# Four convolution layers on one core: chains that use the shared bank in turns, and layer 2's edge columns taken from the loaded chunk

## The chip, the core and the metric

The kernel runs on one core of a Trainium2 chip. The metric is the device time of one execution in microseconds. Before the change three runs took 2754.84, 2755.46 and 2756.58 us; the median is 2755.46 us.

A core has five engines, each with its own queue of instructions that it takes strictly in order: PE (TensorE, the matrix products), DVE (VectorE), ACT (ScalarE), POOL (GpSimd) and SP (SyncE, which here only issues DMA transfers; POOL issues some too). Engines wait for one another through semaphores. PE writes to PSUM, whose banks hold 512 single-precision numbers for each of 128 partitions; DVE and ACT read PSUM, POOL does not.

## The reference

The input `x` has 16 images of 64 channels and 128 x 128 pixels. Four residual layers follow one another, the first three with a group normalization of 32 groups (two channels each), all in single precision:

```python
# --- layer 0: product with the Gram matrix of the normalized image
x = x + _L0_conv_ref(_gn(x), L0_conv_conv_w)   # gram = xf xf^T / N; conv_w (gram xf)
# --- layer 1: |gx| + |gy| of a 3 x 3 Sobel-like filter, channel by channel
x = x + _L1_conv_ref(_gn(x))
# --- layer 2: shift a quarter of the channels left and a quarter right by one column, then a 3 x 3 convolution with bias
x = x + _L2_conv_ref(_gn(x), L2_conv_W, L2_conv_b)
# --- layer 3: 3 x 3 convolution, 1 x 1 convolution, batch normalization over all images, clipped to 0..255
x = x + _L3_conv_ref(_gn(x), ...)
```

`_gn` subtracts a group's mean and divides by its standard deviation, which need the whole image. So each layer of an image waits for sums over the layer before it. The batch normalization of layer 3 needs all 16 images.

## The kernel before

**Tiling.** An image is cut into `NS` = 8 chunks of `R` = 8 rows in each half; a tile has 128 partitions, two times 64 channels. The layers run as software-pipelined stages: `Gram` (the Gram matrix), `Front` (layers 0 and 1), `Layer2` and `Layer3`. A main loop goes over steps, each of four quarters `q` = 0 to 3. In each quarter every stage's `at(i, q)` issues its part of chunk `i`. `Front` starts image `b` at step 15 + 8 b, `Layer2` at 25 + 8 b, `Layer3` at 35 + 8 b, so the three work side by side on different images, and an image takes eight steps. In a quarter Layer3 comes first, then Layer2, then Front. The helper `InOrder` keeps every engine's instructions in the order in which the program issues them: what the code says first on an engine is done first on it.

**Chains.** The scalar work between layers (means, inverse standard deviations, the folded weights of layer 0) is written as Python generators: `gram_chain` for an image's Gram matrix and `coefficients` for the normalizations before layers 2 and 3. `tick()`, called at the end of each quarter, moves every live chain on to its next `yield`. A chain alternates small DVE operations with small products on PE (`small_product`); `rstd` also takes a square root on ACT, named `sd`. The products' results lie in one PSUM bank, `bank`; `sm(n)` hands out its columns. The Gram matrices of the images after the sixth accumulate in the same bank. Reads and writes of the bank by two engines are kept in program order, whichever columns they touch. A Gram chain of a late image waits, after its first DVE read, until step 8 b - 4; its last result, `lead[b]`, is taken by `Front` 13 steps after step 8 b.

**Layer 2.** `load(i + 2)` in quarter 1 fetches a chunk of layer 1's output on SP's queue into a tile `v2` (the profile calls it `v`), shifting the channels by one column on the way. The flat tile is `self.whole[i]`; `self.v[i]` is the part from its second element on. A step later, in quarter 1, ACT normalizes the whole tile in place (`act.activation(f, f, ...)`; `v<-v,co` in the profile). POOL then computes the edge columns that the shift loses: four `tensor_scalar_mul` operations of 64 x 8 elements (`edges<-v,co`), and after them two multiplications by the masks `keep0` and `keep1` on 128 x 9 elements (`v<-v,kc`). The convolution uses differences of rows (`d`, by DVE) and copies of them shifted by a column (`qd`, the `twin`). In layer 2 the twin is made by two DMA transfers on POOL's queue, `twin(0)` in quarter 0 and `twin(1)` at the end of quarter 3. PE computes a shared product (`one`, a single PSUM buffer), which ACT copies to `c`, and two own products (`two`). DVE adds the edges to `two` with two operations of 8 elements a partition, then adds `c` and takes the sum (`x<-two,c`). The sums of squares are ACT's (`junk`).

**Layer 3** has the same form with its own `one`, `two`, `c`, `d`, `qd` (copied by ACT) and `y<-two,c`. **Front** does layer 0 on PE (`po`), normalizes on ACT into `xh`, and computes the Sobel part on DVE (`u`, `e`), with the absolute values on ACT (`u<-u`, `e<-e`). While Gram products run, ACT also turns rows of `x` into columns (`xw<-xr`).

After the last image the batch normalization's sums are finished, and a tail loads layer 3's result and layer 2's output, normalizes, clips, adds and stores.

In the functions below, the change touches `tick`, `coefficients`, `gram_chain` and `Layer2.at`, and adds `when` and `Layer2.sides`.

Of the kernel before, what the change touches and what calls it, by code (L numbers as in the profile page):

```python
# [108 lines left out]
def tile_kernel(ctx: ExitStack, tc: tile.TileContext, x, cw_h, w2_t, b2, wbin_t, w1_t, b1, gamma, beta, consts, out):  # L109
# [143 lines left out]

    now = [0]
    chains = []

    def tick():
        for c in list(chains):
            if next(c, chains) is chains:
                chains.remove(c)  # L260
# [19 lines left out]
    def coefficients(st, put, back=None):  # L280

        s2 = sv("s2", 2)
        dve.tensor_reduce(s2, st, axis=AX.X, op=ALU.add)
        yield
        pm = sm(2)
        small_product(pm, k("gmean"), s2)
        yield
        co = sv("co", 2) if back is None else sv("co2", 6)
        me = sv("me", 2)
        r, mean = co[:, 0:1], me[:, 0:1]  # L290
        yield from rstd(pm, r, me, GN_EPS)
        dve.scalar_tensor_tensor(co[:, 1:2], mean, -1.0, r, op0=ALU.mult, op1=ALU.mult)
        if back is not None:

            dve.reciprocal(co[:, 2:3], r)
            dve.tensor_mul(co[:, 3:4], co[:, 2:3], k("left"))
            dve.tensor_mul(co[:, 4:5], co[:, 2:3], k("right"))
            dve.tensor_add(co[:, 5:6], mean, back)
        put(co)


# [2 lines left out]
    def gram_chain(b, pg):  # L304

        gs = stp.tile([P, C + 1], F32, tag="gs", name=f"gs_{b}", bufs=2)
        if b > 2 * EARLY:
            dve.tensor_reduce(gs, pg.rearrange("p (j c) -> p c j", j=3), axis=AX.X, op=ALU.add)
        else:
            dve.tensor_copy(gs, pg)  # L310
        if b > 1:
            yield
        while b > 2 * EARLY and now[0] < NS * b - 4:
            yield
        gd = sm(C + 1)
        small_product(gd, k("same"), gs)
        yield
# [9 lines left out]
        )  # L327
        if b > 1:
            yield
        pm = sm(2)  # L330
        small_product(pm, k("gavg"), st)
        yield
# [9 lines left out]
            dve.tensor_scalar_mul(dd[:, s, :], k("Id"), vv[:, s:s + 1])  # L342
        if b > 1:
            yield

        pr = sm(2 * C)
        small_product(pr, k("all"), dd.rearrange("p s c -> p (s c)"))
# [9 lines left out]
        csf = cs.rearrange("p s c -> p (s c)")  # L357
        if b > 1:
            yield
        pq = sm(C)  # L360
        small_product(pq, csf, rc)
        yield
# [8 lines left out]
        dve.tensor_add(abd, wbd, k("I"))  # L371
        if b > 1:
            yield
        pd = sm(C + 3)
        small_product(pd[:, 0:C], csf, ad)
        small_product(pd[:, C:C + 2], abd, vv[:, 0:2])
# [7 lines left out]
        dve.tensor_copy(av, pd[:, C:C + 3])  # L384
        if b > 1:
            yield
        pk = sm(1)
        small_product(pk, pp.rearrange("p s c -> p (s c)"), k("q"))
        if b > 1:
# [8 lines left out]
        )  # L398
        if b > 1:
            yield  # L400
        pm = sm(2)
        small_product(pm, k("gavg"), st1)
        yield
# [343 lines left out]
    class Layer2:  # L747
# [7 lines left out]
        def load(self, i):  # L755
# [14 lines left out]
            self.v[i] = t[:, 1:N - 1].rearrange("p (j w) -> p j w", w=W)  # L770
            self.whole[i] = t

        def store(self, i):

            d, t = x3_d[self.b], tiles3[self.b][i]
            for s in range(2):
                v = pairs(d, 1)[:, i * R:(i + 1) * R, :].rearrange("c (n s) w -> c s n w", s=2)
                sp.dma_start(v[:, s], t[hi, s])
            for s in range(2):
                j = i * R + 1 + s  # L780
                m = CP if i + 1 < NS or s == 0 else CP - 1
                if j + 2 * m <= NP:
                    v = pairs(d, 0)[:, j:j + 2 * m, :].rearrange("c (n s) w -> c s n w", s=2)[:, 0]
                else:
                    v = pairs(d, 0)[:, j - 1:j - 1 + 2 * m, :].rearrange("c (n s) w -> c s n w", s=2)[:, 1]
                sp.dma_start(v, t[lo, s, 0:m])
            if i + 1 == NS:
                sp.dma_start(pairs(d, 0)[:, 0:1, :], t[lo, 1, CP - 1:CP])
# [24 lines left out]
        def at(self, i, q):  # L813
# [3 lines left out]
            if q == 0:  # L817
                if i == NS:
                    chains.append(coefficients(self.st, self.done))
                if 1 <= i:  # L820
                    two = self.p.pop(i - 1)[0]

                    e = self.edges.pop(i - 1).rearrange("p t (m n) -> p t n m", n=2)
                    for side, w in ((0, 0), (1, W - 1)):
                        dve.tensor_add(two[:, :, :, w], two[:, :, :, w], e[:, side])
                    x3 = ring.tile([P, 2, CP, W], F32, tag="x3", name=f"x3_{b}_{i - 1}", bufs=NS + 2)
                    tiles3[b].append(x3)
                    dve.scalar_tensor_tensor(
                        x3.rearrange("p s j w -> p s (j w)"), two.rearrange("p s j w -> p s (j w)"), 1.0,
                        self.c.unsqueeze(1).to_broadcast([P, 2, CP * W]),  # L830
                        op0=ALU.mult, op1=ALU.add, accum_out=self.st[:, 0, i - 1:i],
                    )
                if 0 <= i < NS:
                    difference("d2", 0, self.v[i], m)
                    self.twin(0)
            if q == 1:
                if i == 0:

                    self.wi = stp.tile([P, 2, 3, P], F32, tag="wi", name=f"wi_{b}", bufs=1)
                    for n, base in ((0, w2[:, 2]), (1, wm)):  # L840
                        dve.scalar_tensor_tensor(
                            self.wi[:, n].rearrange("p k o -> p (k o)"), k("I3"), self.co[:, 2:3],
                            base.rearrange("p k o -> p (k o)"), op0=ALU.mult, op1=ALU.add,
                        )
                if -1 <= i < NS - 1:
                    if i == -1:
                        self.co = coefs2.pop(b)
                    t, f = self.v[i + 1], self.whole.pop(i + 1)
                    act.activation(f, f, AF.Identity, bias=self.co[:, 1:2], scale=self.co[:, 0:1])


                    e = stp.tile([P, 2, R], F32, tag="edges", name=f"edges_{b}_{i + 1}", bufs=3)
                    for side, at in ((0, 0), (1, W + 1)):
                        for rows, j in ((lo, 1), (hi, 0)):
                            n = at + j * W
                            pool.tensor_scalar_mul(
                                e[rows, side], f[rows, n:n + (R - 1) * W + 1:W], self.co[rows, 3 + side:4 + side]
                            )
                    self.edges[i + 1] = e

                    pool.tensor_scalar_mul(t[:, :, 0], t[:, :, 0], k("keep0"))
                    pool.tensor_scalar_mul(t[:, :, W - 1], t[:, :, W - 1], k("keep1"))
                if i + 2 < NS:
                    self.load(i + 2)
# [28 lines left out]
                        issue([taps(0, p, [w2[:, 0], both], srcs), taps(1, p, [both, w2[:, 1]], srcs)])  # L893
            if q == "first of 3" and 0 <= i < NS:
                self.c = ring.tile([P, CP * W], F32, tag="c2", name=f"c2_{b}_{i}", bufs=1)
                act.activation(self.c, flat(self.p[i][1]), AF.Identity, bias=self.co[:, 5:6])
            if q == "last of 0" and i == NS:
                self.square(i - 1)
            if q == "last of 3" and -1 <= i < NS - 1:
                difference("d2", 1, self.v[i + 1], CP if i + 2 < NS else CP - 1)  # L900
                self.twin(1)


    class Layer3:
# [266 lines left out]
```

## Time and profile before

| what | value |
|---|---|
| median of three runs | 2755.46 us |
| the profiled execution's own time | 2756.86 us |
| its span, first to last instruction | 2755.1 us |
| busy: PE, DVE, ACT, POOL | 2159.6, 2192.4, 2113.5, 943.2 us |
| mean granted clock of PE | 0.896 |
| HBM traffic | 346.23 MB read, 268.44 MB written |
| the `edges` operations on POOL | 512, in all 397.7 us, 0.30 us the shortest, 0.32 the median, 4.46 the longest |
| the edge additions on DVE | 256, 171 ns in the mean |

The profile is of one execution. Busy time is the time in which an engine has an instruction under way; matmuls are pipelined, so PE's is only roughly the time of its work. A wait row tells who waited, for whom, the total in us, the number of times, and the longest. A timeline row tells when an instruction starts, how long it takes, its engine, its output and inputs by the program's names, its shape and how many equal ones were merged; in brackets stands how long the engine was idle before it and what ended that. All instructions of the ordered engines bear one line number, that of the helper, so the names of the tiles tell them apart.

### The profile page before, as it was taken

To read this page: it belongs to the slowest core of one execution; us is meant where nothing else is said; L and a number is where in the kernel's file an instruction comes from. 1 tells how busy PE (TensorE), PEld (TensorE's weight loads), DVE (VectorE), ACT (ScalarE), POOL (GpSimd) and SP (SyncE) were. 2 spreads that over 40 slices of the span, in tenths; PEclk is the share of its full clock that TensorE was granted. 3 is DMA by queue.
4 is the path that set the end of the run, shared out by engine and by line. 5 is a ranking of instruction groups with operands and counts; after the bars stand their busy time and mean duration, and the time that the engine had idled before them with its cause. 6 is when DMAs were issued, how large, how long until landed. Compare 5 with 4: busy or idle time off the path is not lost. (4 is left out here: it accounts for less than half of the span.)

```text
span 2755.1 us, 46091 instructions
## 1 busy us (share of the span) xinstructions
PE 2159.6 (78%) x14804; PEld 886.9 (32%) x14804; DVE 2192.4 (80%) x3623; ACT 2113.5 (77%) x3177; POOL 943.2 (34%) x1350
## 2 busy tenths in 40 slices
PE   6578799999999999999999999999999994000000
PEld 4233333434343434343434343333334641000000
DVE  4998899899999999999999999999996335333332
ACT  4766779998989898989898989899997667333332
POOL 2055444444444444444434444454544300000000
PEclk8689899999999999999999999999999997555555
DMA  8799779898888898888888887888887768999999
GB/s 206 200 229 233 196 183 249 214 244 220 235 224 233 215 240 224 234 227 224 230 228 226 223 203 192 208 207 206 216 207 192 219 191 297 419 420 420 420 420 384
DMA packets 693601, 685.96 MB, mean 249 GB/s; under 512 B 60096, under 2 KB 580448, under 8 KB 693360
## 3 DMA queue, kind: packets, MB, share of 16 engines
q1 hardware_dynamic: 668208, 613.83, 76.0%
q0 software_dynamic: 25152, 69.18, 9.9%
q8 instruction: 119, 1.95, 0.3%
q14 instruction: 122, 1.00, 0.1%
HBM read 346.23 MB, written 268.44 MB: 223 GB/s over the span
## 5 line engine op out<-in xcount | busy, mean ns | idle before, releaser
L73 PE MATMUL two<-d,w 128*64 128x508 f32 (+2 forms) x2560 | 837.5, 587 | 0.0
L73 PE MATMUL two<-d,wi 128*64 128x508 f32 (+3 forms) x1536 | 572.7, 578 | 0.0
L73 POOL DMA_DIRECT2D qd<-d x512 | 270.8, 531 | 851.5 <-issue 295.8
L73 PE MATMUL two<-qd,pk 128*64 128x512 f32 (+1 forms) x1024 | 518.3, 587 | 10.1 <-DMA qd<-d 8.8
L73 POOL TENSOR_SCALAR edges<-v,co 64x8 f32<-64x8 f32 x512 | 397.7, 777 | 287.4 <-ACT v L73 204.0
L73 DVE TENSOR_TENSOR d<-v 128x512 f32<-128x512 f32 (+1 forms) x512 | 346.5, 679 | 58.4 <-issue 29.7
L73 PE MATMUL one<-v,w 128*64 128x508 f32 (+2 forms) x1600 | 364.6, 580 | 30.1 <-ACT c L73 30.1
L73 PEld LDWEIGHTS two<-d,w 128*64 128x64 f32 x2560 | 265.8, 136 | 326.3 <-issue 289.8
L73 PE MATMUL one<-v,wi 128*64 128x508 f32 (+3 forms) x1536 | 360.6, 602 | 1.5 <-issue 1.4
L73 ACT COPY qd<-d 64x512 f32<-64x512 f32 x512 | 315.5, 616 | 18.6 <-DVE d L73 12.5
L73 DVE SCALAR_TENSOR_TENSOR e<-e 128x1032 f32<-128x1032 f32 (+1 forms) x256 | 313.2, 1223 | 0.0
L73 ACT ACTIVATE xh<-po,co 128x128 f32<-128x128 f32 (+1 forms) x480 | 274.9, 621 | 31.0 <-PE po L73 24.9
L73 POOL TENSOR_SCALAR v<-v,kc 128x9 f32<-128x9 f32 x256 | 246.7, 976 | 11.9
L73 ACT ACTIVATE u<-u 128x1024 f32<-128x1024 f32 x128 | 135.7, 1060 | 144.2 <-DVE u L73 144.2
L73 PEld LDWEIGHTS two<-d,wi 128*64 128x64 f32 x1536 | 177.5, 136 | 193.5 <-issue 179.2
L73 ACT ACTIVATE v<-x,co 128x512 f32<-128x512 f32 (+2 forms) x368 | 235.0, 705 | 0.0
L73 DVE SCALAR_TENSOR_TENSOR y<-two,c 128x1024 f32<-128x1024 f32 x128 | 156.0, 1219 | 94.0 <-ACT v L73 68.2
L73 PE MATMUL po<-x,abd 64*64 64x512 f32 (+1 forms) x1024 | 177.7, 641 | 43.9 <-ACT xh L73 41.6
L73 PEld LDWEIGHTS one<-v,w 128*64 128x64 f32 x1600 | 124.6, 136 | 227.9 <-issue 139.5
L73 PEld LDWEIGHTS two<-qd,pk 128*64 128x64 f32 x1024 | 136.0, 136 | 151.1 <-issue 101.9
L73 DVE SCALAR_TENSOR_TENSOR u<-xh 128x1170 f32<-128x1170 f32 x128 | 175.4, 1371 | 4.8 <-ACT xh L73 4.5
L73 PEld LDWEIGHTS one<-v,wi 128*64 128x64 f32 x1536 | 109.3, 139 | 195.9 <-issue 188.3
(165 smaller groups left out, 3321.0 us busy)
## 6 DMA issues: line engine op xcount, KB each, us to landing
x<-in_x SPq DMA_DIRECT2D x256, 256.0 KB, 4.6
x_d<-u SPq DMA_DIRECT2D x512, 128.0 KB, 4.0
y_d<-y SPq DMA_DIRECT2D x512, 128.0 KB, 3.8
x_d<-x SPq DMA_DIRECT2D x496, 128.0 KB, 2.8
xr<-in_x SPq DMA_DIRECT2D x120, 512.0 KB, 6.5
qd<-d POOLq DMA_DIRECT2D x256, 130.0 KB, 3.1
qd<-d POOLq DMA_DIRECT2D x256, 129.8 KB, 3.9
v<-x_d SPq DMA_DIRECT2D x448, 72.1 KB, 2.9
```

Of the source, the lines that this page charges most:

```text
L73: return self.tc.keep_in_program_order(call(*args, **kwargs))
```

## The change

**Turns.** `tick` counts quarters. `when(who)` holds a chain until the count has the right parity: DVE's reads of the bank by the Gram chain start in odd ticks (quarters 0 and 2), the small products in even ones (quarters 1 and 3). All of `gram_chain` from the third image on is put in these turns, and the product in `coefficients`. In `gram_chain` the loop that waits for step 8 b - 4 moves ahead of the first `yield`.

**Edges.** The edge columns are computed from the loaded chunk as it is, before it is normalized: (value - mean) times a mask, in one POOL operation, where before the normalized value was multiplied by a coefficient. The coefficients of layer 2 have five columns for six: the mean is kept, and the two masked inverses go. `sides(i)` does the four POOL operations. For chunk 0 it is called in quarter 0 of the step before the image's first, for the others at the end of quarter 3, one step after the load was issued. The normalization stays in quarter 1 and works in place, so it comes after `sides` of its chunk; the mask multiplications stay behind it. On DVE one operation over both edge columns adds the edges where there were two.

```diff
+    turn_of = [0]
+    VECTOR, TENSOR = 1, 0
+    def when(who):
+        while turn_of[0] % 2 != who:
+            yield
     def tick():
+        turn_of[0] += 1
         for c in list(chains):
...
         dve.tensor_reduce(s2, st, axis=AX.X, op=ALU.add)
         yield
+        yield from when(TENSOR)
         pm = sm(2)
...
             dve.reciprocal(co[:, 2:3], r)
-            dve.tensor_mul(co[:, 3:4], co[:, 2:3], k("left"))
-            dve.tensor_mul(co[:, 4:5], co[:, 2:3], k("right"))
-            dve.tensor_add(co[:, 5:6], mean, back)
+            dve.tensor_copy(co[:, 3:4], mean)
+            dve.tensor_add(co[:, 4:5], mean, back)
...
+        if b > 1:
+            yield from when(VECTOR)
         if b > 2 * EARLY:
             dve.tensor_reduce(gs, pg.rearrange("p (j c) -> p c j", j=3), axis=AX.X, op=ALU.add)
         else:
             dve.tensor_copy(gs, pg)
+        while b > 2 * EARLY and now[0] < NS * b - 4:
+            yield
         if b > 1:
             yield
-        while b > 2 * EARLY and now[0] < NS * b - 4:
-            yield
+            yield from when(TENSOR)
         gd = sm(C + 1)
         small_product(gd, k("same"), gs)
...
+        def sides(self, i):
+            e = stp.tile([P, 2, R], F32, tag="edges", name=f"edges_{self.b}_{i}", bufs=3)
+            for side, at, which in ((0, 0, "left"), (1, W + 1, "right")):
+                for rows, j in ((lo, 1), (hi, 0)):
+                    n = at + j * W
+                    pool.tensor_scalar(
+                        e[rows, side], self.whole[i][rows, n:n + (R - 1) * W + 1:W], self.co[rows, 3:4],
+                        k(which)[rows], op0=ALU.subtract, op1=ALU.mult,
+                    )
+            self.edges[i] = e
...
-                    e = self.edges.pop(i - 1).rearrange("p t (m n) -> p t n m", n=2)
-                    for side, w in ((0, 0), (1, W - 1)):
-                        dve.tensor_add(two[:, :, :, w], two[:, :, :, w], e[:, side])
+                    e = self.edges.pop(i - 1).rearrange("p t (m n) -> p n m t", n=2)
+                    ends = two[:, :, :, 0:W:W - 1]
+                    dve.tensor_add(ends, ends, e)
...
+            if q == 0 and i == -1:
+                self.co = coefs2.pop(b)
+                self.sides(0)
             if q == 1:
...
                 if -1 <= i < NS - 1:
-                    if i == -1:
-                        self.co = coefs2.pop(b)
                     t, f = self.v[i + 1], self.whole.pop(i + 1)
                     act.activation(f, f, AF.Identity, bias=self.co[:, 1:2], scale=self.co[:, 0:1])
-                    e = stp.tile([P, 2, R], F32, tag="edges", name=f"edges_{b}_{i + 1}", bufs=3)
-                    for side, at in ((0, 0), (1, W + 1)):
-                        for rows, j in ((lo, 1), (hi, 0)):
-                            n = at + j * W
-                            pool.tensor_scalar_mul(
-                                e[rows, side], f[rows, n:n + (R - 1) * W + 1:W], self.co[rows, 3 + side:4 + side]
-                            )
-                    self.edges[i + 1] = e
                     pool.tensor_scalar_mul(t[:, :, 0], t[:, :, 0], k("keep0"))
...
             if q == "last of 3" and -1 <= i < NS - 1:
                 difference("d2", 1, self.v[i + 1], CP if i + 2 < NS else CP - 1)
                 self.twin(1)
+                if i + 2 < NS:
+                    self.sides(i + 2)
```

The other places where `yield from when(TENSOR)` goes in are the six further products of `gram_chain`, each after its `yield`.

## The prediction

> **What bounds the kernel now.** I read the granted clock first (0.896 over the span, 1.00 from 500 to 2110 us), then the busy time by stretches, then the waits of each engine, then the timeline of single passes. The columns of the stretches are length, then busy time and instructions of PE, PEld, DVE, ACT and POOL, clock, DMA share, GB/s.
>
> ```profile
> 150.80:500.00 349.20, 302.49 (x2312) 123.75 (x2309) 317.25 (x579) 268.46 (x403) 167.42 (x214) 0.93 0.86 217
> 500.00:1700.00 1200.00, 1177.58 (x8314) 466.24 (x8312) 1143.63 (x1944) 1098.86 (x1716) 520.89 (x746) 1.00 0.86 225
> 2310.00:2755.00 445.00, 0.00 (x0) 0.00 (x0) 154.44 (x128) 154.60 (x127) 0.00 (x0) 0.50 1.01 413
> ```
>
> Three engines are over 90% busy in the middle: PE 98%, DVE 95%, ACT 92%. PE is the bound there, VectorE and ScalarE have a few tenths of a us to spare in each step, and POOL is less than half used. The last 445 us are transfers; the change leaves them alone. Up to 500 us PE has gaps. What ends PE's waits, from 500 to 2100 us and then from 140 to 500 us:
>
> ```profile
> PE one L73 <- ACT c L73: 28.3, 25, 1.9
> PE two L73 <- DMA qd<-d: 2.7, 3, 1.5
> PE bank L73 <- DVE rc L73: 0.4, 1, 0.4
> ...
> PE bank L73 <- DVE dd L73: 7.6, 2, 4.2
> PE bank L73 <- DVE g L73: 7.3, 1, 7.3
> PE bank L73 <- DVE ad L73: 3.8, 2, 2.0
> ```
>
> So in the steady part the shared bank holds PE up for under 1 us in all; the bank rows that matter (24.4 us with three smaller ones: 2.9, 1.4, 1.4) lie early. The one steady wait is for `c`, ScalarE's copy of the shared product: twice an image, where layer 2 passes from one image to the next. I therefore read that place closely, in one image. Step A runs from 1342.83 to 1357.32, B to 1376.73, C to 1391.36 (starts of VectorE's `u<-xh`); A returns each 132.5 us (1475.29). In A layer 2 does its last chunk of one image and prepares chunk 0 of the next.
>
> ```profile
> 1347.18 1.35 ACT L73 ACTIVATE v<-v,co 128x1154 f32<-128x1154 f32 x1
> 1348.02 1.02 POOL L73 DMA_DIRECT2D qd<-d  x2 [6.05 <-issue]
> 1348.42 1.20 ACT L73 COPY xw<-xr 128x1024 f32<-128x1024 f32 x1
> 1349.08 3.90 POOL L73 TENSOR_SCALAR edges<-v,co 64x8 f32<-64x8 f32 x4
> 1350.92 1.06 ACT L73 ACTIVATE u<-u 128x1024 f32<-128x1024 f32 x1 [1.30 <-DVE u L73]
> 1355.07 0.68 ACT L73 ACTIVATE c<-one,co 128x512 f32<-128x512 f32 x1
> 1356.80 0.59 PE L73 MATMUL one<-v,w 128*64 128x512 f32 x1
> ```
>
> Order is what counts: ScalarE normalizes the chunk (`v<-v,co`) at 1347.18, before POOL takes the edges at 1349.08. From 1350.92 ScalarE runs without a gap to the end of A and far into B, where VectorE waits 1.75 us for it (`s<-st <-ACT junk`, 1363.83); from there VectorE, ScalarE's `sd` (1373.14, 1.41 us idle before it) and `c` lead to PE's 1.78 us wait at 1373.97. A delay of ScalarE in A thus comes out at PE.
>
> **The change, part by part.**
>
> *Edges before the normalization, chunk 0 (the part that decides).* `sides(0)` is issued in the first quarter of A, behind the two `qd` transfers of the last chunk on POOL's queue; those wait for VectorE's `d` (1346.90 to 1347.46) and hold POOL until 1349.04. So POOL starts the edges at 1349.08, as it does now, in the same stretch of VectorE work. What changes is who waits: they read the raw chunk, so ScalarE, which overwrites it in place, now waits for them, and behind it in ScalarE's queue stand `xw`, `u`, `e`, `junk`, `xh` and `c`. Four edge operations take 3.90 us there although the shortest takes 0.30: VectorE's two-input operations run back to back until its `y` starts (1351.94). Taking 3.90 us, they end at 1352.98. Two parts pull this earlier: the Gram chain's last seven small operations (1340.50 to 1341.54, some 1.0 us) leave the stretch before A, where VectorE has just waited 1.29 us for PE, and the edge addition is 0.2 us shorter; against it, 0.5 us of the chain now stands before VectorE's sobel work. I take 0.6 us off: 1352.35. Then `v` 1.35 and `xw` 1.20, overlapping by 0.1: `u` starts at 1354.8 instead of 1350.92, 3.9 us late. `c` moves from 1355.07 to about 1359, PE stops 2.9 us at 1356.80, and through the ScalarE and VectorE run in B the whole 3.9 us reaches PE at 1373.97, since nothing in that run is idle but the waits on each other. The granted clock and PE's saturation leave it no way to catch up.
>
> A has an `xw` copy for eight images (at 1342.83 and the seven others while the Gram products run, steps A from 548 to 1475 us): 8 x 3.9 = 31 us. In four later ones there is none: at 1740.92 `v` ran, `u` at 1744.69 after 2.42 us idle, edges 1742.84 plus 3.90 = 1746.74. `v` 1746.7 to 1748.1, `u` 3.3 late, less 0.1 for the shorter addition: 4 x 3.2 = 13 us. Three early ones: edges end at 158.48, 283.71 and 427.06; `u` at 157.28, 280.77 and 424.89 becomes about 2.5, 4.2 and 3.9 later (10.6; the last is 4.6 less part of the 1.65 us that POOL idles there); engines are partly idle there, so between 0 and 10.6, taken 7. The sixteenth image has no front work beside it: 0. Sum +51; bounds: 0 if a cover that I don't see exists, and 12 x 4.5 + 10.6 = 65 without the 0.6 us.
>
> The Trainium skill, "SBUF — State Buffer", section "Who interferes with whom", says that a VectorE operation with two SBUF inputs and a GpSimd one that reads SBUF exclude one another for a whole instruction, and that whoever issued first goes first. By that rule alone an edge operation would wait for at most the rest of one 1.2 us VectorE operation, the four would end near 1352.3, and the part above would be about 7 us less; the row shows them held until the one-input `y`, and the row is used.
>
> *Edges of the other chunks.* `sides(i + 2)` stands behind the second pair of `qd` issues (1391.73 to 1392.8 at the end of C) and needs the chunk's load: six issues from 1385.32 to 1388.20, and 2.9 us to landing by the page, hence 1391.1, in time. In B it is 1357.08 + 2.9 = 1360.0 against POOL free at 1358.78: 1.2 us of waiting. POOL then has VectorE's edge addition and `x<-two,c` (about 1.4 us, few SBUF reads) for four operations of 0.39 us pitch: they fit, end some 4 us into a step, and ScalarE's `v` comes at 6.3 (1383.01, C) to 9.0 (1366.35, B). Behind them on POOL is the `qd` issue at 1382.04, which PE needs at 1387.29: 1383.06 + 3.9 to landing leaves 0.3 us. Taken 0; lower bound 0 (PE can't run faster), upper as in rival 2. The mask multiplications `v<-v,kc` come earlier in their step, which removes VectorE's waits for them (3.1 us in 11); PE bounds there, so 0. A two-operation POOL instruction isn't in the trace with this shape; the one-operation row has 0.30 us at least and 0.32 median, the 128x9 multiplication 0.98 mean; taken 0.32, since the shape is the same.
>
> *One edge addition for two.* 2 x 171 ns become one of 16 elements, at 0.17 (an 8-element row) to 0.34: 128 x 0 to 0.17, at most 22 us of VectorE. PE bounds most of it; taken -2, for the chunks before 400 us.
>
> *Turns.* The tick parity is fixed: first and third quarters are VectorE's, second and fourth PE's. Coefficient chains already ran that way, so their dates stay; one product of two less on VectorE (0.15 us an image), inside waits. Gram chains from the seventh image on start a quarter later, end two quarters later, in the first two of A, many steps before `lead` is popped: 0 for PE (its bank waits there sum to under 1 us). ScalarE's `sd` now waits in A and in an earlier step at the end of the first quarter; in A that lies inside the wait for POOL, in the other inside the 1.25 us that ScalarE has idle before `u` at 1431.33. The early images gain. At 298.57 the product of a coefficient chain had waited 7.34 us for a read by another chain:
>
> ```profile
> 298.57 0.38 PE L73 MATMUL bank<-s,kc 128*64 128x2 f32 x4 [7.34 <-DVE g L73]
> ...
> 306.34 0.16 DVE L73 COPY me<-bank 128x2 f32<-128x2 f32 x1 [6.28 <-PE bank L73]
> ```
>
> Its own input was ready at 292.76. With turns that read falls in the next quarter: -7.3, as all three engines stood. The other 17.1 us of bank waits shift with the phases; VectorE is the bound there (317 of 349 us), so between 0 and 17; taken 3. Together -10. No wait of the loop is an added instruction: `when` only dates what is issued.
>
> Sum: +31 + 13 + 7 - 2 - 10 = +39. Span 2755.1, the profiled execution 2756.86; 2796 against it, and against the median 2755.46, which is 1.4 lower, 2795.
>
> **Rivals.** 1, faster: chunk 0's delay is covered, and the early bank waits go. ScalarE is idle 1.30 us (2.42 in later images) before `u`; the cover holds if the edges end by about 1347.2, before POOL even starts them, or if PE had slack behind `c`, which the 1.1 us from 1355.7 to 1356.80 gives only without the run in B. Price -10 to -24, less 2: 2729 to 2743. 2, much slower: loads land late, or edges take two slots of VectorE's work. If the fourth edge is still waiting when `x<-two,c` ends, it is held into sobel, up to `y` at 1385.96, and the `qd` issue goes from 1382.04 to 1386.3; landing 1391.2, PE stops 3.9 us. One chunk in four of 84: +82, 2877; one in eight: 2836. For it: the 0.3 us of slack; against it: landings ahead of POOL in the rows read. 3, a small loss: B's stop absorbs part of A's (it is 1.78 us already), and early gains reach 17: +5 to +22, 2760 to 2777. 4, neither: both cancel, 2750 to 2761.
>
> **How the numbers follow.** Within 0.2% (5.5 us) a measurement of this kernel can't tell a change. Forecast (2777 to 2820): 0.59. Rival 1: 0.10. Rival 2: 0.13, of which about half is below 2832. Rival 3: 0.12. Rival 4: 0.06, nearly all within 0.2%. Faster 0.10, same 0.06, slower 0.84. The range goes from 2757, taking in rival 3, to 2832; left out are rival 1 and half of rival 2.
>
> **What would show it.** Right: in each A, ScalarE's `v<-v,co` waits about 5 us for POOL's edges and starts 9 to 10 us into the step; PE's wait for `c` shows a new entry of about 3 us at the end of A; an image takes 136 us instead of 132.5. The 7.34 us wait at 298 is gone. Wrong: `v` in A starts before the edges end, or A to A stays at 132.5; or `two <- DMA qd<-d` grows past 20 us, which is rival 2. A POOL operation of 0.6 us instead of 0.32 would break the fit of the other chunks.

## The result, and the profile after

The changed kernel takes 2823.7 us (median of four runs, 2820.53 to 2828.94) against 2755.8 us before: 68 us more, ratio 1.0251, 95% interval 1.0238 to 1.0264. The forecast was 2795 us, with a range from 2757 to 2832. The direction and the named place were right; some 29 us of the loss lie in a place that the forecast had set to zero.

The profiled execution took 2828.94 us, its span is 2827.2 us. The stretches, with the same columns as before; the last is the tail of 445 us, later by as much as the span is longer:

```profile
150.80:500.00 349.20, 295.61 (x2262) 124.97 (x2260) 309.31 (x551) 260.31 (x394) 164.57 (x212) 0.93 0.84 215
500.00:1700.00 1200.00, 1140.45 (x8046) 444.73 (x8044) 1076.79 (x1779) 1049.63 (x1640) 532.23 (x706) 0.99 0.83 216
2382.00:2827.00 445.00, 0.00 (x0) 0.00 (x0) 154.69 (x128) 154.85 (x127) 0.00 (x0) 0.50 1.01 414
```

The tail is untouched. In the middle PE is busy 1140 us of 1200 where it was 1178, and all three engines do less: the pipeline waits. What ends PE's waits, from 500 to 2100 us and then from 140 to 500 us:

```profile
PE one L73 <- ACT c L73: 55.5, 34, 3.4
PE two L73 <- DMA qd<-d: 20.8, 12, 2.7
...
PE two L73 <- DMA qd<-d: 22.1, 7, 4.9
PE bank L73 <- DVE rc L73: 2.7, 1, 2.7
```

Two rows have grown in the steady part: the wait for `c` from 28.3 to 55.5 us, and the wait for `qd` from 2.7 to 20.8. The second passes the 20 us that the prediction had named as the sign of its second rival. Early, the bank's longest row has gone from 7.6 to 2.7 us, while `qd` went from 6.1 to 22.1.

Step A of the same image as before now runs from 1386.54 to 1404.64, 18.10 us instead of 14.49:

```profile
1391.53 1.03 POOL L73 DMA_DIRECT2D qd<-d  x2 [4.61 <-issue]
1392.59 5.03 POOL L73 TENSOR_SCALAR edges<-v,co,kc 64x8 f32<-64x8 f32 x4
1397.65 1.35 ACT L73 ACTIVATE v<-v,co 128x1154 f32<-128x1154 f32 x1 [3.57 <-POOL edges L73]
1399.94 1.05 ACT L73 ACTIVATE u<-u 128x1024 f32<-128x1024 f32 x1
1403.88 0.67 ACT L73 ACTIVATE c<-one,co 128x512 f32<-128x512 f32 x1
1404.61 4.41 PE L73 MATMUL one<-v,w 128*64 128x512 f32 x12 [2.33 <-ACT c L73]
```

This is the chain of the prediction: edges at the old time, `v<-v,co` behind them, `u` at 13.40 us into the step instead of 8.09, `c` late, and PE stopped for `c` at the end of A. Two steps after B comes a place that the prediction did not look at. Step C begins at 1425.47, the one after it, here called D, at 1439.88. D in the changed kernel:

```profile
1440.25 1.08 POOL L73 DMA_DIRECT2D qd<-d  x2 [5.23 <-DVE d L73]
1442.55 0.20 POOL L646 MEMSET xh<- 64x130 f32 x1 [1.21 <-DVE two L73]
1442.84 6.36 POOL L73 TENSOR_SCALAR edges<-v,co,kc 64x8 f32<-64x8 f32 x4
1449.14 1.10 POOL L73 DMA_DIRECT2D qd<-d  x2
1454.25 0.61 PE L73 MATMUL two<-qd,pk 128*64 128x512 f32 x1 [2.13 <-DMA qd<-d]
```

and the same step D before (it starts at 1391.36):

```profile
1391.73 1.08 POOL L73 DMA_DIRECT2D qd<-d  x2 [1.99 <-DVE d L73]
1394.03 0.20 POOL L629 MEMSET xh<- 64x130 f32 x1 [1.21 <-DVE two L73]
1396.67 1.03 POOL L73 DMA_DIRECT2D qd<-d  x2 [2.44 <-DVE d L73]
1400.49 2.04 POOL L73 TENSOR_SCALAR edges<-v,co 64x8 f32<-64x8 f32 x4 [2.78 <-DMA y_d<-y]
```

A `memset` of one row of Front's tile, which stands outside the ordered queues, is placed between the second pair of `qd` transfers and the edges. By its row it waits for VectorE's edge addition. In the kernel before nothing stood behind it but twin(0), which had 2.44 us to spare. Now the edges do: they start 2.96 us into D, meet VectorE's Sobel work, take 6.36 us, and push twin(0) from 5.3 to 9.3 us into the step. PE stops 2.13 us. In the step after D a second memset of this kind stands in the same place (at 1457.76, after 1.12 us of waiting), and there the edges take 5.32 us.

### The profile page after: what moved, and what is told of

It reads as the page before. It is cut to its first block, busy times and chain, and to the rows that moved or that the text cites. A ratio compares the mean times of both kernels' runs of the same rounds, so it can differ in the third digit from the quotient of the medians.

```text
span 2827.2 us, 45815 instructions
## 1 busy us (share of the span) xinstructions
PE 2177.5 (77%) x14804; PEld 885.1 (31%) x14804; DVE 2169.2 (77%) x3479; ACT 2108.5 (75%) x3177; POOL 995.0 (35%) x1350
## 5 line engine op out<-in xcount | busy, mean ns | idle before, releaser
L73 PE MATMUL two<-d,wi 128*64 128x508 f32 (+3 forms) x1536 | 579.6, 582 | 0.0
L73 POOL DMA_DIRECT2D qd<-d x512 | 279.1, 546 | 844.8 <-DVE d L73 543.3
L73 POOL TENSOR_SCALAR edges<-v,co,kc 64x8 f32<-64x8 f32 x512 | 512.4, 1001 | 88.8 <-DVE co L73 42.5
L73 PE MATMUL one<-v,w 128*64 128x508 f32 (+2 forms) x1600 | 376.5, 599 | 60.9 <-ACT c L73 60.9
L73 PE MATMUL one<-v,wi 128*64 128x508 f32 (+3 forms) x1536 | 351.8, 589 | 2.9 <-DVE wi L73 1.5
L73 POOL TENSOR_SCALAR v<-v,kc 128x9 f32<-128x9 f32 x256 | 178.0, 706 | 237.6 <-ACT v L73 237.6
L73 ACT ACTIVATE v<-v,co 128x1154 f32<-128x1154 f32 x128 | 172.2, 1345 | 116.3 <-POOL edges L73 108.2
L73 DVE SCALAR_TENSOR_TENSOR u<-xh,co,u 128x1024 f32<-128x1024 f32 x128 | 163.9, 1280 | 60.6 <-ACT u L73 60.5
```

The costliest lines, as they stand in the source:

```text
L73: return self.tc.keep_in_program_order(call(*args, **kwargs))
```

## The experiments

All differences are against the median of runs of the kernel before that were made beside each kernel (2755.8 to 2756.9 us). Step lengths are means over the nine images between 529 and 1718 us (times of before), from the starts of VectorE's `u<-xh`; E is the step after D.

```
kernel           difference  ratio (95%)              A      B      C      D      E     image
before                  -    1                      14.49  19.31  14.63  14.88  15.59  132.16
after                +67.9   1.0251 (1.0238-1.0264) 18.01  20.73  14.50  15.30  15.60  138.15
turns_only            -7.1   0.9972 (0.9962-0.9982) 15.92  19.32  14.63  14.88  15.10  132.69
turns_merged         -15.3   0.9946 (0.9934-0.9959) 15.72  19.32  14.44  14.95  15.12  132.56
turns_early          -21.4   0.9923 (0.9910-0.9937) 14.29  19.27  14.43  14.86  15.47  131.83
edges_only           +82.1   1.0300 (1.0286-1.0314) 17.92  20.72  14.50  15.32  15.42  138.59
chunk0_after         +14.0   1.0051 (1.0037-1.0064) 15.72  19.27  14.50  15.32  15.51  134.11
sides0_first         +18.8   1.0072 (1.0058-1.0086) 15.80  19.24  14.50  15.30  15.63  134.40
chunk0_after_sp      +57.0   1.0206 (1.0192-1.0220) 15.97  19.34  15.22  16.23  15.35  136.16
chunk0_memset         -9.0   0.9971 (0.9960-0.9982) 15.76  19.24  14.50  14.40  14.91  132.50
sides0_memset         -3.7   0.9985 (0.9976-0.9995) 15.75  19.24  14.50  14.55  14.95  132.19
one_op               +27.4   1.0100 (1.0085-1.0115) 17.36  20.73  14.38  14.41  14.91  135.39
delay5               +50.1   1.0183 (1.0170-1.0197) 16.70  20.77  14.63  14.88  15.59  136.00
delay4               +35.1   1.0130 (1.0113-1.0147) 15.69  20.72  14.63  14.88  15.60  134.95
```

**The two halves of the change.** `turns_only` is the kernel before with `when`, `tick`'s count and the turns in the chains, nothing else.

> The turns alone on the kernel before; edges and edge additions as they were. By the prediction's term -10: 2745 us, with the 7.34 us wait at 298 us gone and an image still at 132.5 us. Rival: the turns cost time in the steady part (the chain's small VectorE operations and its square root now stand ahead of the step's own work), and the loss of the whole change is partly theirs: an image over 134 us, 2765 us or more. Between: within 3 us of the time before, if the early gain is given back by later waits.

Measured 2749.6 us, -7.1: between the first case (2745) and the third (within 3 us of the time before). The bank's waits from 140 to 500 us fall from 24.4 to 5.2 us in all, and the step that began at 528.8 us begins at 517.3. After that 0.5 us an image is given back: A is 1.4 us longer, and other steps win a part of it back.

`edges_only` is the change without the turns.

> The edge part alone (raw chunk, sides, one addition), chains without turns. If turns and edges only add up, and the turns are worth -10: about 2834 us. If the turns cost nothing in the steady part and gain nothing early: 2824 us, as with both. If the turns are a part of the loss: 2800 us or less. Steps A should be 3 to 4 us longer here as well, with the normalization waiting for the edges.

Measured 2838.8 us, +82.1, 5 us above the first case; A is 3.4 us longer than before, as expected. So the whole loss is the edge part's, and the turns are not part of it: 82.1 - 7.1 is 75, the whole change 67.9. Together the two are 7 us better than their sum.

**Chunk 0 alone.** `chunk0_after` takes back the early `sides` for chunk 0 only; the two masked inverses come back as columns 5 and 6 of the coefficients:

```diff
             if q == 0 and i == -1:
                 self.co = coefs2.pop(b)
-                self.sides(0)
...
                     act.activation(f, f, AF.Identity, bias=self.co[:, 1:2], scale=self.co[:, 0:1])
+                    if i == -1:
+                        e = stp.tile([P, 2, R], F32, tag="edges", name=f"edges_{b}_0", bufs=3)
+                        for side, at in ((0, 0), (1, W + 1)):
+                            for rows, j in ((lo, 1), (hi, 0)):
+                                n = at + j * W
+                                pool.tensor_scalar_mul(
+                                    e[rows, side], f[rows, n:n + (R - 1) * W + 1:W], self.co[rows, 5 + side:6 + side]
+                                )
+                        self.edges[0] = e
```

> The whole change, but the edges of chunk 0 alone are taken as before, from the normalized chunk and behind it (two small VectorE products for the coefficients come back). If the wait of ScalarE for POOL in step A is the cause: step A back to 14.5 us, an image at 132 to 133.5 us, 2750 to 2772 us. If the other chunks' edges carry the loss (the late transfer for twin(0) in one step of each image, 1.5 to 2.7 us, and the normalization behind the edges): an image at 135 us or more, 2785 us or more. No step with PE at half clock is expected if the wait for c in A no longer reaches 2.3 us.

Measured 2770.8 us. The loss of 67.9 shrinks by 53.9 to 14.0, and an image from 138.15 to 134.11. A and B are back to the lengths of the turns alone. So chunk 0 is the larger cause by far, as the prediction had it; but an image is still 1.4 us longer than with the turns alone, and `two <- DMA qd` stays at 18.3 us from 500 to 2100 us. That remainder is the second cause. One expectation failed: PE has seven stretches at half clock between 500 and 2100 us here too (more on them in the last section).

`sides0_first` keeps all edges on the raw chunk and only issues chunk 0's ahead of twin(0) of the chunk before on POOL:

```diff
+                if stage is Layer2 and q == 0:
+                    for b in range(B):
+                        i = step - at - NS * b
+                        if i == -1:
...
+                            live[Layer2, b].co = coefs2.pop(b)
+                            live[Layer2, b].sides(0)
                 for b in range(B):
                     run(stage, b, step - at - NS * b, q)
...
             if q == 0 and i == -1:
-                self.co = coefs2.pop(b)
-                self.sides(0)
```

> The whole change, but the edges of chunk 0 are issued ahead of the last chunk's twin(0) on POOL, that is at the start of step A instead of 5 us into it. If only their place in POOL's queue matters: they end some 5 to 6 us into A, the normalization starts there, 5 us earlier than with the change, the loss of 6.2 us an image shrinks to 0 to 2: 2755 to 2785 us. Rival: VectorE's two-input operations at the start of A hold them as long, twin(0) stands behind them, and its transfer is late: PE waits for qd in A, and the time stays above 2805 us.

Measured 2775.5 us, within the first theory's range. POOL and ScalarE in its step A (it starts near 1355):

```profile
1355.57 4.13 POOL L73 TENSOR_SCALAR edges<-v,co,kc 64x8 f32<-64x8 f32 x4
1360.15 1.11 POOL L73 DMA_DIRECT2D qd<-d  x2 [0.44 <-issue]
...
1362.61 1.34 ACT L73 ACTIVATE v<-v,co 128x1154 f32<-128x1154 f32 x1
```

The four operations take nearly as long, but they end 2.9 us before ScalarE comes to the chunk, and no wait is left. The price of chunk 0's edges was where they stood in two queues, not the operation.

**What a late ScalarE in A costs by itself.** `delay5` and `delay4` are the kernel before with five or four idle squares behind that normalization, once an image:

```diff
                     act.activation(f, f, AF.Identity, bias=self.co[:, 1:2], scale=self.co[:, 0:1])
+                    if i == -1:
+                        for _ in range(5):
+                            act.activation(junk, f[:, 0:R * W], AF.Square)
```

> The kernel before, with five more ScalarE operations (squares of 128x1024 into the scratch tile, about 1.05 us each) behind the normalization in step A, once an image: no edge is moved and POOL is not touched. It measures what a late ScalarE in A costs by itself. ScalarE had 1.30 us idle there (2.42 later), so u is 3.95 us late (2.8). By the prediction's rule that the whole delay reaches PE: 8 x 3.95 + 4 x 2.8 + 0 to 10 at the start: 2798 to 2809 us. Rival, half of it is absorbed by the stop in step B: 2775 to 2785 us. Rival, PE's clock falls to half after the stop and this costs 1.7 us more each time: 2815 us or more.

> As delay5 with four operations instead of five, so ScalarE's u in A is some 2.9 us late (1.8 in the later images) and PE's new stop in A shrinks from 2.36 us to about 1.3, below every stop that was seen to halve PE's clock. If the price is only the delay: 8 x 1.05 + 4 x 1.05 + 0 to 3 = 13 to 16 us less than delay5, 2791 to 2794 us. If each of the twelve half-clock stretches of 3.4 us in delay5 costs PE up to 1.7 us, they go too: 2771 to 2785 us.

Measured 2807.0 and 2791.5 us, each in its first case. The timeline of `delay5`:

```profile
1377.61 1.34 ACT L73 ACTIVATE v<-v,co 128x1154 f32<-128x1154 f32 x1
1378.98 5.41 ACT L73 ACTIVATE junk<-v 128x1024 bf16<-128x1024 f32 x5
1384.30 1.14 ACT L73 COPY xw<-xr 128x1024 f32<-128x1024 f32 x1
1385.33 1.05 ACT L73 ACTIVATE u<-u 128x1024 f32<-128x1024 f32 x1
1390.01 2.36 PE L73 MATMUL one<-v,w 128*64 128x512 f32 x10 [2.37 <-ACT c L73]
```

From `v` to `u` it is 7.72 us here and 3.74 in the kernel before: `u` is 3.98 us late, and an image is 3.84 us longer. One operation fewer (1.08 us by the row of five) makes an image 1.05 us shorter and the kernel 15.4. So ScalarE's delay in A reaches the end almost one to one, in A and B together, without any edge being moved. That is the rule on which the prediction's 51 us stood. The stop in B does not swallow it.

**The edges of the other chunks.** Three runs look into the remainder that `chunk0_after` leaves; the first two start from that kernel, the third from the whole change. `chunk0_after_sp` lets SyncE issue the transfers of twin(0), so that no edge stands before them.

```diff
-            pool.dma_start(flat(q[cols(i), n]), flat(d[cols(i), n]))
-            pool.dma_start(
+            by = pool if n else sp
+            by.dma_start(flat(q[cols(i), n]), flat(d[cols(i), n]))
+            by.dma_start(
```

> The kernel chunk0_after (edges of chunk 0 as before, the others from the raw chunk) with the transfers of twin(0) issued by SyncE instead of POOL, so that they no longer stand behind the edges. If the 21 us that chunk0_after has over the turns alone come from the late transfer: two <- DMA qd from 18 us to under 5, and 2750 to 2756 us. If they come from the normalization behind the edges (ScalarE's wait for POOL, 25.8 us in all, 4.0 at most): 2765 us or more. If SyncE's queue holds the loads of chunks behind the twin, PE or POOL waits for loads, and it gets slower than 2771 us.

Measured 2813.9 us: the third case. `two <- DMA qd` falls to 5.9 us, but by the order of the code the transfers now stand in SyncE's queue until VectorE's `d` is there, with the chunk loads behind them. What POOL's edges wait for (us in all, times), in `chunk0_after` and then in `chunk0_after_sp`:

```profile
  DMA v<-x_d: 7.5, 5
...
  DMA v<-x_d: 150.7, 70
```

The run shows how little room the loads had, and does not by itself settle the 29 us. (In the code a chunk's load and its `sides` stand in the same step, in quarter 1 and at the end of quarter 3; the section on the change has them one step apart.)

`chunk0_memset` is `chunk0_after` with the two memsets of `xh` put in POOL's program order:

```diff
-                nc.gpsimd.memset(self.chunk(0)[lo, 0, :], 0.0)
+                pool.memset(self.chunk(0)[lo, 0, :], 0.0)
...
-                    nc.gpsimd.memset(self.chunk(NS - 1)[hi, R + 1, :], 0.0)
+                    pool.memset(self.chunk(NS - 1)[hi, R + 1, :], 0.0)
```

> The kernel chunk0_after, with the two memsets of a row of xh on POOL put where the program has them (behind the masks, in the third quarter). In chunk0_after one of them stands between the second pair of qd transfers and the edges, waits for VectorE's edge addition, and starts the edges 1.2 us later, in the stretch of VectorE's two-input operations; there twin(0) goes out late and PE waits for qd once an image (18.3 us in all, at most 2.7). If this memset is what breaks the fit: two <- DMA qd falls under 4 us and the time to 2748 to 2755 us, 18 us less. Rival, the edges don't fit by themselves (0.41 us each): the waits for qd stay, 2765 us or more.

Measured 2747.5 us, 23 us less than `chunk0_after`. Its step D starts near 1384.5:

```profile
1384.84 1.09 POOL L73 DMA_DIRECT2D qd<-d  x2 [5.22 <-DVE d L73]
1385.97 4.32 POOL L73 TENSOR_SCALAR edges<-v,co,kc 64x8 f32<-64x8 f32 x4
1390.24 1.11 POOL L73 DMA_DIRECT2D qd<-d  x2
```

Without the memset in front the edges start 1.5 us into D instead of 2.96 and end in time for twin(0): it goes out 5.7 us into the step, 0.4 us later than before the change (5.3), and D and E are shorter by 0.9 and 0.6 us. The waits for `qd` fall from 18.3 us (14 times) to one of 3.1. So the memset is what broke the fit. It is worth 23 of the 29 us. Of the 6 that are left against `turns_merged` (below), 5 lie in the start: the step that began at 528.8 us begins at 519.6 here and at 514.2 there.

`one_op` is the whole change with the mask multiplication left out of POOL's instruction; the memset and chunk 0 stay as in the change:

```diff
-                    pool.tensor_scalar(
-                        e[rows, side], self.whole[i][rows, n:n + (R - 1) * W + 1:W], self.co[rows, 3:4],
-                        k(which)[rows], op0=ALU.subtract, op1=ALU.mult,
-                    )
+                    pool.tensor_scalar_sub(
+                        e[rows, side], self.whole[i][rows, n:n + (R - 1) * W + 1:W], self.co[rows, 3:4]
+                    )
```

> The whole change with one operation in POOL's edge instruction instead of two: only the mean is subtracted, the multiplication by the channel mask is left out, so the edge addition adds values that it should not. It tells whether the two-operation form (407 ns in the median against 318) matters. If the fit of the other chunks breaks by those 0.09 us x 4: the waits for qd go and the time falls by 15 to 20 us, to 2804 to 2810 us. If it only shortens the wait in step A by 0.1 to 0.4 us an image: 2819 to 2823 us. If VectorE's operations set the end of the edges anyway: no change, 2823 us.

Measured 2783.9 us: 40 us less than the change, more than any of the three cases. The durations of the edge operations (minimum, median, maximum in ns), first of the whole execution, of the change and then of `one_op`, next of the four in step D, in the same order, and `one_op`'s step D:

```profile
L73 POOL TENSOR_SCALAR edges<-v,co,kc x512: 392/407/4936, 150.8 to 2270.9; 64x8 f32<-64x8 f32 x171
...
L73 POOL TENSOR_SCALAR edges<-v,co x512: 302/313/2503, 149.4 to 2223.4; 64x8 f32<-64x8 f32 x171
...
L73 POOL TENSOR_SCALAR edges<-v,co,kc x4: 395/1344/3031, 1442.8 to 1446.9; 64x8 f32<-64x8 f32 x4
...
L73 POOL TENSOR_SCALAR edges<-v,co x4: 304/310/1712, 1412.0 to 1413.1; 64x8 f32<-64x8 f32 x4
```

```profile
1411.72 0.20 POOL L646 MEMSET xh<- 64x130 f32 x1 [1.21 <-DVE two L73]
1412.00 2.86 POOL L73 TENSOR_SCALAR edges<-v,co 64x8 f32<-64x8 f32 x4
1414.92 1.10 POOL L73 DMA_DIRECT2D qd<-d  x2
```

With the memset in front of them, and starting as late as in the change, four one-operation instructions take 2.86 us where four of the other form took 6.36. The form's own 0.09 us is not the whole difference. Taken one by one, three of the four in `one_op` are done before VectorE's Sobel run begins, and the fourth takes 1.71 us. In the change only two are done by then; the third takes 3.03 us and the fourth 2.28, and both end 0.1 to 0.2 us after one of VectorE's operations in that run ends. Of the 40 us some 13 come before the step that starts at 535 us with the change (522 here); the rest is 2.76 us an image: 0.65 in A, 0.9 in D, 0.7 in E, 0.5 in others.

Either cure is enough for D: no memset, or one operation. The change had both the longer form and the memset in the way.

`sides0_memset` joins the two orders, `sides0_first` and the memsets in program order.

> The kernel sides0_first (all edges from the raw chunk, chunk 0's ahead of the last chunk's twin(0)) with the two memsets in the program's order. If the order on POOL is all that was wrong with the edges from the raw chunk: two <- DMA qd from 22.6 us to under 4, and 2752 to 2759 us; then 10 to 18 us are left against turns_merged (2741.5), for the startup, the longer POOL operations and ScalarE's waits. If the memset isn't the cause: 2770 us or more.

Measured 2752.7 us, with runs from 2745 to 2758. All edges come from the raw chunk here, in the two-operation form, and the loss is gone, the wait for `qd` being down to 3.7 us from 500 to 2100 us: a change of the order on POOL is enough to take away the 68 us. Against `turns_merged` some 12 us are left; the image is 132.19 us, so they lie in the start (526.7 against 514.2 us for the same step).

**The parts that gain.** `turns_merged` has the turns and the one edge addition, and takes the edges as before.

> The turns and the one edge addition, edges taken from the normalized chunk as before. By the prediction's term the addition is worth -2 against the turns alone: 2747 to 2748 us. Rival: it gives up to 0.17 us in each of the chunks where VectorE bounds (mod-5, -6, -7 steps and the start): 2740 us or less. If it gives nothing: 2749.6 us.

Measured 2741.5 us, 8 us less than the turns alone: nearer to the rival (2740 or less) than to the term. By the starts of the same steps, 3 us of it are there at 517 us, 4 at 1711, and all of it at Front's last step (2059.0 us against 2067.2), so half comes in the last images.

`turns_early` keeps the old dates for the Gram chains of the late images (cut against `turns_merged`; the loop that waits for step 8 b - 4 also goes back behind the first `yield`):

```diff
+        late = b > 2 * EARLY
+        def turn(who):
+            if not late:
+                yield from when(who)
...
-            yield from when(TENSOR)
+            yield from turn(TENSOR)
```

> As turns_merged, but only the first seven images' Gram chains run in turns; those of the later images, whose VectorE work the turns moved into step A (15.92 us for 14.49 in the mean of nine images), keep their old dates. If the turns gain early (11.5 us by step starts at 517 us against 529) and lose 0.5 us an image later, the loss goes: 4 us less than turns_merged, about 2744 us. Rival: the step lengths only shift the same idle time about, and nothing changes: within 1.5 us of turns_merged.

Measured 2735.5 us, 6 us less than `turns_merged` and 21.4 less than the kernel before (ratio 0.9923, 0.9910 to 0.9937). It beats both kernels. Step A shows why the turns cost late images time. First VectorE, then ScalarE in `turns_merged`:

```profile
1334.48 0.56 DVE L73 TENSOR_TENSOR d<-v 128x384 f32<-128x384 f32 x1
1334.95 0.15 DVE L73 COPY co<-bank 128x2 f32<-128x2 f32 x1
...
1335.46 1.23 DVE L73 SCALAR_TENSOR_TENSOR u<-u 128x1040 f32<-128x1040 f32 x1
...
1335.58 0.20 ACT L73 ACTIVATE sd<-nv 128x1 f32<-128x1 f32 x1 [1.86 <-DVE nv L73]
1338.06 1.34 ACT L73 ACTIVATE v<-v,co 128x1154 f32<-128x1154 f32 x1
```

The chain's square root now sits in ScalarE's queue in A and waits 1.86 us for three small VectorE operations; the normalization starts 7.45 us into A where it started at 4.34. In `turns_early` A is 14.29 us again.

## Why the prediction was right, and where it was not

By differences, the change is made up of four parts: turns -7.1, the one addition -8.2 (`turns_merged` less `turns_only`), the edges of the other chunks +29.3 (`chunk0_after` less `turns_merged`), chunk 0 +53.9 (the change less `chunk0_after`). Each was measured with the ones before it in place; they sum to +67.9 by construction. The prediction had -10, -2, 0 and +51.

*Chunk 0, forecast +51, measured +53.9: right in mechanism, in size partly by luck.* ScalarE's `v<-v,co` waits for POOL and starts 11.1 us into A (forecast 9 to 10), PE's new stop for `c` is 2.3 us (about 3), the wait in B grows too, and the delays by themselves cost what was assumed. The wait for POOL itself is 3.57 us, not about 5, since `sd` has already held ScalarE for 1.64 us.

Two terms inside were off, in opposite directions. The 0.6 us taken off the end of the edges did not come: they end 11.08 us into A instead of 9.52. The chain's small operations in A are not the reason, for without the turns (`edges_only`) the edges end at 11.02. The two-operation form is a part of it: in `one_op` they end at 10.45, and the first instruction takes 2.42 us where that of the change takes 3.56. So `u` starts 5.31 us later than before the change, not 3.9. The other term is `sd`: with the turns the comparison is no longer `u` at 8.09 us but at about 9.8, since without edges in front the square root's wait alone puts it there. What the edges add to that is 3.65 us; an image became 4.04 longer (138.15 less 134.11). Without the turns the edges make A and B together 4.8 us longer (`edges_only` less the kernel before). That the sum came out near 51 is the luck of two errors that nearly cancel.

The Trainium skill, "SBUF — State Buffer", section "Who interferes with whom", would have each POOL operation wait for one VectorE instruction at most. The 3.56 us operation does not agree with that: it began behind VectorE's instruction of 1392.55, and VectorE began two further ones of 1.2 us meanwhile (1393.69 and 1394.83). Nor does the row of before agree. The prediction read its four operations as held until `y`; taken one by one they end at 1350.99, 1352.21, 1352.59 and 1352.98. The first came through within VectorE's run, but only after the rest of one instruction and the whole of the next (1349.67 to 1350.89). The end near 1352.3 that the prediction gives for the page's rule is an estimate whose working it does not show.

*Edges of the other chunks, forecast 0, measured +29: wrong.* The failed step is the fit: "they fit, end some 4 us into a step". In B and C, the two steps that the prediction read, it holds; the edges end 4.75 and 4.68 us into them. In D a memset stands in front. It was in the trace of before at 1394.03, with its 1.21 us of waiting, but the timeline was read from A to C, and only instructions of the code under change were counted on POOL's queue. Reading one image from end to end would have shown it. Rival 2 had the mechanism (the fourth edge held into Sobel, twin(0) 4 us late, PE stops) at a chance of 0.13. Its price was higher, a stop of 3.9 us where 2.13 was measured, or 41 us for one chunk in eight; its trigger was another; and the 0.3 us of slack for twin(0), which the prediction named, was what it used up. The duration of a two-operation instruction, bounded by 0.32 and 0.98 us and taken at the lower end, was 0.41. This is the other half of the same error, as `one_op` shows: the point from which the fit breaks had been put at 0.6, without the memset.

*One edge addition, forecast -2, measured -8: the sign right, the size too small.* "PE bounds most of it" left out the last images: 4 us of the 8 come after 1711 us.

*Turns, forecast -10, measured -7.* The 7.34 us wait went, and 11.5 us were gained by 517 us, so the early term was right. "0 for PE" in the steady part was wrong by 0.5 us an image: ScalarE's `sd` was taken to lie "inside the wait for POOL", which it does only as long as that wait is there.

*The remaining claims.* An image takes 138.15 us, not 136: 4.04 from chunk 0, 1.55 from the other chunks, 0.4 from turns and addition. The rivals 1, 3 and 4 needed a cover for chunk 0's delay; the delay runs show that there is none.

## What to carry to other kernels

A step moved on an in-order queue meets everything that is on that queue, also what is placed there outside the code being edited: follow the queue through a whole period of the pipeline, not through the steps that look like the bound. When one engine overwrites a buffer in place, a reader that moves ahead of it hands its whole waiting time to that engine's queue; issue the reader where it can be done before the writer comes, as `sides0_first` did. Parts of a change are worth separating: two parts of this one save 21 us, when the turns are kept to the images in which the bank's waits are on the path.

## What the runs showed of the hardware

*PE's clock falls after stops of about 2 us.* In the kernel before PE's granted clock is 1.00 from 500 to 2110 us; its longest stop for `c` there is 1.9 us. In several of the others stretches of 3.4 us at 0.50 appear behind stops of some 2 us and more, though not behind each. The 3.4 us after step B's stop are shown first for the kernel before (stop 1.78 us), then for `turns_merged` (2.14 us); the count behind the second figure is that of PE's matmuls, the clock is the third figure from the end:

```profile
1374.00:1377.40 3.40, 3.40 (x16) 1.18 (x18) 3.23 (x11) 3.34 (x6) 1.08 (x2) 1.00 0.79 219
```

```profile
696.91 4.48 PE L73 MATMUL one<-v,w 128*64 128x512 f32 x12 [2.14 <-ACT c L73]
...
697.70:701.10 3.40, 3.40 (x10) 0.98 (x8) 3.23 (x12) 3.34 (x6) 1.09 (x2) 0.50 0.59 135
```

10 matmuls fall in it instead of 16. The price is small. In `turns_merged` the images (from step B to step B) with such a stretch behind the stop take 133.15 to 133.20 us and two without it 132.79 and 132.83, so 0.4 us; in `turns_only` it is the same, 133.34 and 133.37 against 132.95 to 133.02, though its stops there are all of 2.17 us. (The image that begins near 1080 us is left out; it is half a us longer in `turns_early` too, which has no such stretch after 500 us.) `delay5` has twelve such stretches between 400 and 2250 us and `delay4` seven, and the two differ by no more than the operation that was taken out; but within `delay4` the price shows again, 135.49 to 135.57 us for five images with a stretch against 135.07 and 135.33 for two without. Where it follows a stop in D it cost more, 136.73 us against 134.1 to 134.8 for other images of `chunk0_after`; there is one such image among the nine of that run and there are two in the change (139.9 and 140.0 against 137.2 to 138.7), so the loss of 68 us holds a few us of it at most.

The Trainium skill, "TensorE: Matmul & The Clock Gate", Part 1, section "What's actually happening", puts the fall to half rate after at least one idle window of about 3.4 us. The stretch has that length here, but a stop of 2.14 us was enough, with 1.46 us of PE work in the 3.6 us around it. What decides is not shown: of the eight stops of 2.17 us for `c` in `turns_only` between 500 and 2100 us, four were followed by such a stretch and four were not.

*How long POOL is held beside VectorE depends on the instruction's form.* The same 64 x 8 elements with one operation or two take 0.31 and 0.41 us when free. When they meet VectorE's run of two-input operations the four take 2.86 and 6.36 us (step D). The held ones of the longer form took 3.56 us in A, 3.03 and 2.28 in D, those of the shorter form 2.42 and 1.15 in A, 1.71 in D. Why the longer form is held longer was not measured; it was read in the images shown here.
